# Two graph layers on one core: watched sums on GpSimd, the last fold and bias placed anew, the adjacency turned on VectorE

## The chip, the cores and the metric

The kernel runs on one core of a Trainium2 chip. The core has five engines with instruction queues of their own: TensorE (PE) multiplies matrices into PSUM, VectorE (DVE), ScalarE (ACT) and GpSimd (POOL) work elementwise, and SyncE (SP) issues all the transfers here. Each engine takes its instructions strictly in the order in which they were written; semaphores order the engines among each other. The metric is the device time of one launch in microseconds, the median of three runs. Times inside the profile count from the start of its span.

## The reference

There are B = 32 graphs of N = 512 nodes with D = 512 features, and one 512 x 512 adjacency of zeros and ones (symmetric here, with a full diagonal). Layer 0 is attention with 8 heads of 64, masked by the adjacency; layer 1 sums over neighbours and applies a weight. Both end in a residual and a layer norm.

```python
# layer 0, per graph
q, k, v = (x @ W + b for W, b in ((Wq, bq), (Wk, bk), (Wv, bv)))   # 8 heads of 64
scores = q @ k.T / 8 + where(adj == 0, -1e9, 0)
x = layernorm(x + softmax(scores) @ v)
# layer 1
y = adj @ x
x = layernorm(x + y @ weight + bias)
```

Everything is float32.

## The kernel before, in words

A fast kernel does the whole work and keeps a verdict; a slow general kernel runs only if the verdict says that an input was out of the fast kernel's range (sums of exponentials or their reciprocals too large, or an adjacency that a shortened number format doesn't hold exactly). With these inputs it doesn't run.

*Products.* Each 512 x 512 x 512 product is done by Strassen's scheme in 2 x 2 blocks of 256 with seven block products (`project` for q, k and v, `convolve` for layer 1, all through `block_product`, L350). Their factors are blocks or sums of blocks of the weights (`sum_weights`, L302: T1 = B12 - B11, T2 = B22 - T1, T3 = B22 - B12, T4 = B21 - T2) and of the activations (`combine_rows`, L315, on GpSimd but for the first graph). `ORDER` gives the order of the products: 1, 5, 6, 7, 2, 3, 4. The layer-1 products take 1, 2, 5, 6, 7, 3, 4.

*Attention.* Heads go in groups of four, two groups a graph, in pairs hp. `scores` (L558) makes transposed scores, VectorE adds the mask from `gap` (1 where the adjacency is zero) on the way out of PSUM (L560), ScalarE takes the exponential (L562), and GpSimd adds up the exponentials of a pair (L573). `attend` (L582) multiplies with the values. `fold_squares` turns the sums of exponentials in 32 x 32 squares and reduces them (L619, L621), a store and four loads through DRAM bring the partial sums to the right partitions (L626, L633), and `add_up` (L638 to L641) makes the sums and their reciprocals; it also adds both to the running tiles `sums` (VectorE) and `inverses` (GpSimd) for the verdict.

*Layer 1.* `split` cuts the normalised rows into a high and a low half[...] (L438 on ScalarE, L442 on VectorE), and adds the bias of layer 1 to the rows on GpSimd (L443). `aggregate` (L469) multiplies with `adjT`. For the last graph `split_rows` (L488, L489), `add_bias` (L492) and `aggregate_rows` (L501, L506, L508) do this by rows.

*Order.* There is no planner. The main loop writes `attend` and `scores` for each group and then a hand-made list of units (`units_of`, L756): the projections of graph b+1 and the layer-1 work of b-1, with small work of the other engines merged behind each product. For the last graph the first slot holds the layer-1 products of graph 29 with statistics, normalisation, splits and the first fold of the last group behind them (L770); the second slot begins with the second fold and its loads (L771). After the loop stands the end: `add_up`, `last_residual`, the products of graph 30 (`rest`) with the statistics, normalisation and row splits of graph 31 between them, the statistics of graph 29 (`older`), the bias of graph 31, `judge` (L668, the verdict's operands), the aggregation of graph 31, its products (`last`) and the stores of the last rows.

*Start.* Seven matmuls on a zero tile come first. x of graph 0 comes in four transfers, Wq in two column halves of 512 KB (L256), then Wk, held back by a copy on ScalarE (L695), the adjacency in one transfer (L700), Wv, the rows of graph 1 in 16 transfers of squares (L250), x again, the layer-1 weight and x of graph 1. `adjacency(c)` transposes four 128 x 128 blocks on TensorE into PSUM (L284), copies them to `adjT` on ScalarE (L285) and fills `gap` on VectorE (L286).

Of the kernel before, what the change touches and what calls it, by code (L numbers as in the profile page):

```python
# [37 lines left out]
FP = mybir.dt.float32  # L38
# [26 lines left out]
def load_row(nc, pool, v, name):  # L65
    t = pool.tile([P, v.shape[0]], FP, name=name)
    nc.sync.dma_start(t, bass.AP(tensor=v.tensor, offset=v.offset, ap=[[0, P], [1, v.shape[0]]]))
    return t
# [139 lines left out]
def fast_kernel(ctx: ExitStack, tc, verdict, x, adj, Wq, bq, Wk, bk, Wv, bv, W1, b1, out):  # L208
# [16 lines left out]
    def bank(*shape):  # L225

        return psum.tile([P, *shape], FP, name="bank", tag="bank", bufs=8)
# [15 lines left out]
    def load_squares(b):  # L243


        for d in range(DB):
            IN[b, d] = work.tile([P, N // SQ, SQ], FP, name="xin", bufs=XIN)
            for i in range(P // SQ):
                cols = x[b, :, d * P + i * SQ:d * P + (i + 1) * SQ]
                nc.sync.dma_start(IN[b, d][i * SQ:(i + 1) * SQ, :, :], cols.rearrange("(j r) f -> r j f", r=SQ))  # L250
# [10 lines left out]
    wq = load_factors(Wq, "wq")  # L261
# [9 lines left out]
    sums = consts.tile([P, NB, GROUP], FP, name="sums")  # L271
    inverses = consts.tile([P, NB, GROUP], FP, name="inverses")
    nc.gpsimd.memset(sums, 0.0)
    nc.gpsimd.memset(inverses, 0.0)
# [6 lines left out]
    def adjacency(c):  # L281
        pt = bank(NB, P)
        for m in range(NB):
            nc.tensor.transpose(pt[:, m, :], adj_s[:, c, m * P:(m + 1) * P], ident)  # L284
        nc.scalar.activation(adjT[:, :, c * P:(c + 1) * P], pt, AF.Copy)  # L285
        nc.vector.tensor_scalar(gap[:, :, c * P:(c + 1) * P], pt, 0.0, None, op0=ALU.is_equal)  # L286

    def look_for_low_half(c):

        kept = work.tile([P, N], FR, name="high")  # L290
        nc.scalar.activation(kept, adj_s[:, c, :], AF.Copy)
        cut = work.tile([P, N], FP, name="attT")
        nc.vector.tensor_tensor(cut, adj_s[:, c, :], kept.bitcast(FP), op=ALU.not_equal)
        nc.vector.tensor_reduce(inexact[:, c:c + 1], cut, axis=AX.X, op=ALU.add)
# [145 lines left out]
    def split_low(b, d):  # L440
        cols = X[b][:, :, d * P:(d + 1) * P]
        nc.vector.tensor_sub(LOW[b, d], cols, HIGH[b, d].bitcast(FP))  # L442
        nc.gpsimd.tensor_add(cols, cols, b1_r[:, None, d * P:(d + 1) * P].to_broadcast([P, NB, P]))  # L443
# [191 lines left out]
    def add_up(b, g):  # L635

        inverse = INVERSE[b, g] = work.tile([P, NB, GROUP], FP, name="inverse")
        nc.vector.tensor_reduce(inverse, PART.pop((b, g)).rearrange("p a c h -> p c h a"), axis=AX.X, op=ALU.add)  # L638
        nc.vector.tensor_add(sums, sums, inverse)  # L639
        nc.vector.reciprocal(inverse, inverse)  # L640
        nc.gpsimd.tensor_add(inverses, inverses, inverse)  # L641
# [26 lines left out]
    def judge():  # L668
        seen = consts.tile([P, 3], FP, name="seen")
        nc.vector.tensor_reduce(seen[:, 0:1], sums, axis=AX.XY, op=ALU.add)  # L670
        nc.vector.tensor_reduce(seen[:, 1:2], inverses, axis=AX.XY, op=ALU.add)
        nc.vector.tensor_reduce(seen[:, 2:3], inexact, axis=AX.X, op=ALU.add)
        well = consts.tile([P, 3], FP, name="well")
        nc.vector.tensor_scalar(well[:, 0:2], seen[:, 0:2], BOUND, None, op0=ALU.is_le)
        nc.vector.tensor_scalar(well[:, 2:3], seen[:, 2:3], 0.0, None, op0=ALU.is_equal)
        nc.vector.tensor_mul(well[:, 0:1], well[:, 0:1], well[:, 1:2])
        nc.vector.tensor_mul(well[:, 0:1], well[:, 0:1], well[:, 2:3])
        return well[:, 0:1]
# [20 lines left out]
    adj_s = work.tile([P, NB, N], FP, name="yT", bufs=1)  # L699
    nc.sync.dma_start(adj_s, adj.rearrange("(c p) m -> p c m", p=P))  # L700
    wv = load_factors(Wv, "wv")
    bv_r = load_row(nc, consts, bv, "bv_r")
    if B > 1:
        load_squares(1)
# [17 lines left out]
    combine(wv, bv_r)  # L722
    for c in range(NB):
        adjacency(c)
        run(first[9 + c:10 + c])
    run(first[13:16])
# [29 lines left out]
    def units_of(b):  # L756
# [7 lines left out]
        if b == B - 1:  # L764


            first, second = folds(b, 1)
            fetched = [(fetch_parts, b, 1)]
            behind = [fresh[:2], fresh[2:], young[:1] + scaled[:1], young[1:3], young[3:5] + [first],
                      young[5:] + splits[:1], splits[1:] + scaled[1:]]  # L770
            return [merge(convolution(b - 2), behind), [second] + fetched + added + gathered]  # L771
# [64 lines left out]
    run(rest[:1])  # L836
    for c in range(NB):
        statistics(t, 0, c)
    ahead = norm(t, 0)
    run(ahead[:1] + rest[1:2] + ahead[1:2])  # L840
    for c in range(NB):
        run(ahead[2 + c:3 + c])
        split_rows(t, c)
        run(rest[2 + c:3 + c])
    run(rest[2 + NB:])
    older, seen = survey(t - 2), survey(t - 1)
    run(older)
    for c in range(NB):
        add_bias(t, c)
# [53 lines left out]
    store(t, [2, 3])  # L903
# [24 lines left out]
```

## Time and profile before

| | us |
|---|---|
| median of 3 runs | 2744.57 (2743.18 to 2746.03) |
| the profiled execution's own time | 2743.55 |
| its span | 2741.70 |
| PE busy in the span | 2720.6 |
| DVE busy | 2145.6 |
| POOL busy | 1914.2 |
| ACT busy | 1411.0 |

A line of the timeline reads: start, length, engine, source line, operation, output from input, shapes, how many in a row; in brackets how long the engine stood idle before it and what released it. A line of the waits reads: the engine and tile that waited, for whom, microseconds in total, how often, the longest. PEld is the loading of TensorE's stationary operand. The granted clock is TensorE's, 1.00 at full speed. A matmul of float32 appears as two records.

### The profile page before, as it was taken

Reading aid. Unit: us, or ns where it says so; the run is one execution under the profiler, and the core shown is the slowest. Engines: PE = TensorE matmul, PEld = TensorE weight load, DVE = VectorE, ACT = ScalarE, POOL = GpSimd, SP = SyncE. Lnnn points to the kernel's source line nnn. Section 1 sums busy time; section 2 is a strip of 40 time slices with the busy share of each in tenths; the row PEclk is TensorE's granted clock in tenths of the full one; section 3 lists DMA queues with packets and bytes.
Section 4 is the critical chain, followed back from the end, with each engine's and each line's share of the span. In section 5 each row is a group of like instructions: output and inputs, shape, how many; then the busy total and the mean of one; then the engine's idle time right before and its main releaser. Section 6 shows DMA issues by size and latency. Waiting matters only on the chain.

```text
span 2741.7 us, 36328 instructions
## 1 busy us (share of the span) xinstructions
PE 2720.6 (99%) x12344; PEld 1903.7 (69%) x12344; DVE 2145.6 (78%) x3540; ACT 1411.0 (51%) x2459; POOL 1914.2 (70%) x1221
## 2 busy tenths in 40 slices
PE   9999999999999999999999999999999999999997
PEld 6676676766766767667677676676776766767765
DVE  6878778788787787877877778778778787787787
ACT  3455464555544655545545455464465544655554
POOL 4776677766867667777677766686766867767774
PEclk9999999999999999999999999999999999999998
DMA  5223231233221332212323123331233222332121
GB/s 159 49 36 79 69 74 36 60 79 75 67 44 56 75 79 63 54 51 71 79 67 63 45 64 79 71 71 39 61 76 77 65 48 55 72 79 64 48 63 48
DMA packets 632927, 179.16 MB, mean 65 GB/s; under 512 B 578464, under 2 KB 582560, under 8 KB 632736
## 3 DMA queue, kind: packets, MB, share of 16 engines
q1 hardware_dynamic: 632736, 176.79, 27.3%
q8 instruction: 99, 1.62, 0.2%
q14 instruction: 92, 0.75, 0.1%
HBM read 108.01 MB, written 68.68 MB: 64 GB/s over the span
## 4 chain that ended last, share of the span: by engine, by line
PE 96%; DVE 2%; DMA 0%; ACT 0%; POOL 0%; issue 0%; SPq 0%; DVEq 0%; ACTq 0%
PE bank L350 56%; PE bank L558 17%; PE bank L582 16%; PE bank L469 8%; DVE bnst L412 0%; DVE e L560 0%; DMA wq<-in_L_gnn_Wq_dram 0%; DVE xs L531 0%; DVE xT L531 0%; DVE k L442 0%; POOL xs L529 0%; ACT xs L427 0%; DVE sums L639 0%; DVE stat L413 0%; DVE part L861 0%
## 5 line engine op out<-in xcount | busy, mean ns | idle before, releaser
L562 ACT ACTIVATE e<-e 128x1024 f32<-128x1024 f32 x512 | 524.9, 1053 | 575.2 <-DVE e L560 539.9
L573 POOL TENSOR_TENSOR es<-e 128x1024 f32<-128x1024 f32 x128 | 316.5, 2473 | 481.1 <-ACT e L562 481.1
L560 DVE SCALAR_TENSOR_TENSOR e<-gap,bank 128x512 f32<-128x512 uint8 x1024 | 617.7, 678 | 20.2 <-PE bank L558 20.2
L573 POOL TENSOR_TENSOR es<-es,e 128x1024 f32<-128x1024 f32 x256 | 618.9, 2418 | 20.1
L558 PE MATMUL bank<-q,k 64*128 64x512 f32 x2048 | 463.7, 598 | 0.0
L582 PE MATMUL bank<-e,v 128*64 128x512 f32 x2048 | 453.6, 595 | 0.0
L350 PE MATMUL bank<-wv,xT 128*128 128x256 f32 x1792 | 405.4, 381 | 0.0
L350 PE MATMUL bank<-xT,wk 128*128 128x256 f32 x1792 | 402.8, 379 | 0.0
L350 PE MATMUL bank<-xT,wq 128*128 128x256 f32 x1792 | 400.8, 381 | 1.2 <-DMA wq<-in_L_gnn_Wq_dram 1.0
L350 PE MATMUL bank<-w,yT 128*128 128x256 f32 x1792 | 392.6, 379 | 2.7 <-DVE yT L506 2.7
L350 PEld LDWEIGHTS bank<-wv,xT 128*128 128x128 f32 x1792 | 337.7, 190 | 70.2 <-DVE e L560 24.3
L350 PEld LDWEIGHTS bank<-xT,wq 128*128 128x128 f32 x1792 | 337.8, 190 | 69.9 <-DVE e L560 23.5
L558 PEld LDWEIGHTS bank<-q,k 64*128 64x128 f32 x2048 | 203.8, 186 | 258.3 <-issue 147.8
L350 PEld LDWEIGHTS bank<-w,yT 128*128 128x128 f32 x1792 | 340.1, 190 | 51.4 <-DVE yT L506 3.1
L350 PEld LDWEIGHTS bank<-xT,wk 128*128 128x128 f32 x1792 | 340.2, 190 | 46.1
L652 ACT ACTIVATE rows<-rows,zero,inverse 128x64 f32<-128x64 f32 x1008 | 343.1, 426 | 2.1 <-DVE inverse L640 2.1
L582 PEld LDWEIGHTS bank<-e,v 128*64 128x64 f32 x2048 | 141.3, 137 | 277.1 <-issue 275.7
L562 ACT ACT_TABLE_LOAD x30 | 38.5, 1283 | 406.1 <-DVE e L560 406.1
L442 DVE TENSOR_TENSOR low<-xs,high 128x512 fp32r<-128x512 f32 x122 | 163.1, 1337 | 61.5 <-ACT high L438 61.5
L531 DVE TENSOR_TENSOR xs<-bank,xs 128x512 f32<-128x512 f32 x186 | 124.3, 683 | 96.6 <-PE bank L350 57.2
L427 ACT ACTIVATE xs<-xs,shift,rstd 128x512 f32<-128x512 f32 x248 | 181.9, 803 | 32.0 <-DVE shift L422 21.3
L443 POOL TENSOR_TENSOR xs<-xs,b_r 128x512 f32<-128x512 f32 x124 | 157.4, 1282 | 21.5 <-DVE low L442 21.5
(125 smaller groups left out, 3013.0 us busy)
## 6 DMA issues: line engine op xcount, KB each, us to landing
turned<-attT SPq DMA_DIRECT2D x126, 256.0 KB, 2.0
rows<-turned SPq DMA_DIRECT2D x504, 64.0 KB, 2.5
xin<-in_x_dram SPq DMA_DIRECT2D x496, 64.0 KB, 2.4
xs<-in_x_dram SPq DMA_DIRECT2D x31, 1024.0 KB, 5.2
out_dram<-xs SPq DMA_DIRECT2D x31, 1024.0 KB, 4.4
part<-passed SPq DMA_DIRECT2D x256, 8.0 KB, 1.8
passed<-part SPq DMA_DIRECT2D x64, 32.0 KB, 1.5
xin<-in_x_dram SPq DMA_DIRECT2D x4, 256.0 KB, 3.2
```

The source lines that it names most:

```text
L350: nc.tensor.matmul(pm[:, r, :], left[:, d, r * P:(r + 1) * P], right[:, d, :], start=(d == 0), stop=(d == 1))
L427: nc.scalar.activation(row, row, AF.Identity, bias=SHIFT[t][:, slot:slot + 1], scale=RSTD[t][:, slot:slot + 1])
L442: nc.vector.tensor_sub(LOW[b, d], cols, HIGH[b, d].bitcast(FP))
L443: nc.gpsimd.tensor_add(cols, cols, b1_r[:, None, d * P:(d + 1) * P].to_broadcast([P, NB, P]))
L469: nc.tensor.matmul(pm.rearrange("p a n -> p (a n)"), part, adjT[:, n % NB, :], start=(n == 0), stop=(n == 2 * NB - 1))
L531: nc.vector.tensor_add(block, pm, block)
L558: nc.tensor.matmul(ps[s], keys[:, j * P:(j + 1) * P], queries, start=True, stop=True)
L560: nc.vector.scalar_tensor_tensor(e[:, s, :], gap[:, j, :], NEG * root, ps[s], op0=ALU.mult, op1=ALU.add)
L562: nc.scalar.activation(e, e, AF.Exp, scale=1.0 / root)
L573: nc.gpsimd.tensor_add(ES[b, hp], ES[b, hp] if j > 1 else E[b, hp, 0], E[b, hp, j])
L582: nc.tensor.matmul(po[s * HD:(s + 1) * HD, :], values, e[:, s, :], start=(j == 0), stop=(j == NB - 1))
L652: nc.scalar.activation(part, part, AF.Identity, bias=zero, scale=inverse[:, c, s:s + 1])
```

## The change

- `wq` is loaded in four blocks of 256 x 256, in the order B11, B12, B22, B21, in place of two halves.
- The adjacency is loaded as 32 x 32 squares in 16 transfers, as the rows of graph 1 are, and behind Wv and its bias instead of ahead of them. `adjacency(c)` turns a block with one VectorE transpose from SBUF to SBUF; ScalarE and VectorE read that tile. TensorE's sixteen transposes go. One projection unit goes ahead of the first block where the first block stood ahead of it.
- `add_up` puts sum and reciprocal side by side in one tile, and one GpSimd addition adds both to a tile `watched` in place of the two tiles.
- For graph 30 the bias is no longer added in `split_low`, but after the last group's statistics, by rows.
- The second fold of the last group and its loads stand between the second and the third split of graph 30. They stood behind all the layer-1 products of graph 29.
- At the end the first product of graph 30 is written behind the statistics and that bias; `older` and graph 31's bias are spread among the row splits; `judge` reduces both watched rows in one operation and combines the three comparisons by a minimum in place of two multiplications.
- Of the last two row blocks the fourth is stored first.

```diff
+    def place_squares(t, rows, d):
+        for i in range(P // SQ):
+            cols = rows[:, d * P + i * SQ:d * P + (i + 1) * SQ]
+            nc.sync.dma_start(t[i * SQ:(i + 1) * SQ, :, :], cols.rearrange("(j r) f -> r j f", r=SQ))
...
-    wq = load_factors(Wq, "wq")
+    wq = consts.tile([P, 7, 2, half], FP, name="wq")
+    for name, r, c in (("B11", 0, 0), ("B12", 0, 1), ("B22", 1, 1), ("B21", 1, 0)):
+        nc.sync.dma_start(wq[:, B_AT[name], :, :], Wq[r * half:(r + 1) * half, c * half:(c + 1) * half].rearrange(
+            "(c p) f -> p c f", p=P))
...
     def adjacency(c):
-        pt = bank(NB, P)
-        for m in range(NB):
-            nc.tensor.transpose(pt[:, m, :], adj_s[:, c, m * P:(m + 1) * P], ident)
-        nc.scalar.activation(adjT[:, :, c * P:(c + 1) * P], pt, AF.Copy)
-        nc.vector.tensor_scalar(gap[:, :, c * P:(c + 1) * P], pt, 0.0, None, op0=ALU.is_equal)
+        turned = work.tile([P, N], FP, name="attT")
+        nc.vector.transpose(turned, adj_s[:, c, :, :].rearrange("p j f -> p (j f)"))
+        nc.scalar.activation(adjT[:, c, :], turned, AF.Copy)
+        nc.vector.tensor_scalar(gap[:, c, :], turned, 0.0, None, op0=ALU.is_equal)
...
         nc.vector.tensor_sub(LOW[b, d], cols, HIGH[b, d].bitcast(FP))
-        nc.gpsimd.tensor_add(cols, cols, b1_r[:, None, d * P:(d + 1) * P].to_broadcast([P, NB, P]))
+        if b != B - 2:
+            nc.gpsimd.tensor_add(cols, cols, b1_r[:, None, d * P:(d + 1) * P].to_broadcast([P, NB, P]))
...
     def add_up(b, g):
-        inverse = INVERSE[b, g] = work.tile([P, NB, GROUP], FP, name="inverse")
-        nc.vector.tensor_reduce(inverse, PART.pop((b, g)).rearrange("p a c h -> p c h a"), axis=AX.X, op=ALU.add)
-        nc.vector.tensor_add(sums, sums, inverse)
-        nc.vector.reciprocal(inverse, inverse)
-        nc.gpsimd.tensor_add(inverses, inverses, inverse)
+        both = work.tile([P, 2, NB, GROUP], FP, name="inverse")
+        total, inverse = both[:, 0, :, :], both[:, 1, :, :]
+        nc.vector.tensor_reduce(total, PART.pop((b, g)).rearrange("p a c h -> p c h a"), axis=AX.X, op=ALU.add)
+        nc.vector.reciprocal(inverse, total)
+        nc.gpsimd.tensor_add(watched, watched, both)
+        INVERSE[b, g] = inverse
...
     def judge():
-        nc.vector.tensor_reduce(seen[:, 0:1], sums, axis=AX.XY, op=ALU.add)
-        nc.vector.tensor_reduce(seen[:, 1:2], inverses, axis=AX.XY, op=ALU.add)
+        nc.vector.tensor_reduce(seen[:, 0:2], watched.rearrange("p k c h -> p k (c h)"), axis=AX.X, op=ALU.add)
...
-        nc.vector.tensor_mul(well[:, 0:1], well[:, 0:1], well[:, 1:2])
-        nc.vector.tensor_mul(well[:, 0:1], well[:, 0:1], well[:, 2:3])
-        return well[:, 0:1]
+        nc.vector.tensor_reduce(well[:, 3:4], well[:, 0:3], axis=AX.X, op=ALU.min)
+        return well[:, 3:4]
...
-    adj_s = work.tile([P, NB, N], FP, name="yT", bufs=1)
-    nc.sync.dma_start(adj_s, adj.rearrange("(c p) m -> p c m", p=P))
     wv = load_factors(Wv, "wv")
     bv_r = load_row(nc, consts, bv, "bv_r")
+    adj_s = work.tile([P, NB, N // SQ, SQ], FP, name="yT", bufs=1)
+    for c in range(NB):
+        place_squares(adj_s[:, c, :, :], adj, c)
...
+    run(first[9:10])
     for c in range(NB):
         adjacency(c)
-        run(first[9 + c:10 + c])
-    run(first[13:16])
+        run(first[10 + c:11 + c])
+    run(first[14:16])
...
-                      young[5:] + splits[:1], splits[1:] + scaled[1:]]
-            return [merge(convolution(b - 2), behind), [second] + fetched + added + gathered]
+                      young[5:] + splits[:1], splits[1:2] + [second] + fetched + splits[2:] + scaled[1:]]
+            return [merge(convolution(b - 2), behind), added + gathered]
...
-    run(rest[:1])
     for c in range(NB):
         statistics(t, 0, c)
+    for c in range(NB):
+        add_bias(t - 1, c)
+    run(rest[:1])
     ahead = norm(t, 0)
     run(ahead[:1] + rest[1:2] + ahead[1:2])
+    older, seen = survey(t - 2), survey(t - 1)
     for c in range(NB):
         run(ahead[2 + c:3 + c])
         split_rows(t, c)
+        if c == 0:
+            add_bias(t, c)
+        if c == 2:
+            run(older[:2])
         run(rest[2 + c:3 + c])
-    run(rest[2 + NB:])
-    older, seen = survey(t - 2), survey(t - 1)
-    run(older)
-    for c in range(NB):
-        add_bias(t, c)
+        if c > 0:
+            add_bias(t, c)
+    run(rest[2 + NB:] + older[2:])
     well = judge()
...
-    store(t, [2, 3])
+    store(t, [3, 2])
```

## The prediction

> **What bounds the kernel now.** I read the page first. Its first part says who is busy, and the waits of TensorE (PE) say how much of the rest can be won.
>
> ```profile
> PE 2720.6 (99%) x12344; PEld 1903.7 (69%) x12344; DVE 2145.6 (78%) x3540; ACT 1411.0 (51%) x2459; POOL 1914.2 (70%) x1221
> ```
>
> ```profile
> PE bank L501 <- DVE low L489: 3.2, 1, 3.2
> PE bank L350 <- DVE yT L506: 2.7, 1, 2.7
> PE bank L690 <- DVE attT L687: 1.1, 1, 1.1
> PE bank L350 <- DMA wq<-in_L_gnn_Wq_dram: 1.0, 1, 1.0
> PE bank L469 <- DVE low L442: 0.8, 1, 0.8
> PE bank L350 <- DVE wq L302: 0.2, 1, 0.2
> ```
>
> PE never waits between about 11 us and 2679 us. So edits that run in the 32 loops (the sums moved to GpSimd) are worth nothing there: PE hides them. What the change can win or lose lies in the first 45 us and the last 65 us. I took the timeline of both. Start:
>
> ```profile
> 8.30 1.97 PE L350 MATMUL bank<-xT,wq 128*128 128x256 f32 x8 [0.97 <-DMA wq<-in_L_gnn_Wq_dram]
> 9.75 0.69 DVE L302 TENSOR_TENSOR wq<-wq 128x512 f32<-128x512 f32 x1 [1.33 <-DMA wq<-in_L_gnn_Wq_dram]
> 10.49 7.17 PE L350 MATMUL bank<-xT,wq 128*128 128x256 f32 x32 [0.23 <-DVE wq L302]
> 38.34 7.21 PE L558 MATMUL bank<-q,k 64*128 64x512 f32 x32
> ```
>
> End (the third line is one of 1.1 us pieces in which a tiny VectorE (DVE) operation waits for GpSimd (POOL)):
>
> ```profile
> 2681.50 3.48 DVE L442 TENSOR_TENSOR k<-xs,k 128x512 fp32r<-128x512 f32 x2
> 2692.18 0.26 DVE L638 TENSOR_REDUCE inverse<-part 128x16 f32<-128x64 f32 x1 [3.50 <-DMA part<-passed]
> 2692.47 1.09 DVE L639 TENSOR_TENSOR sums<-sums,inverse 128x16 f32<-128x16 f32 x1
> 2703.79 0.77 PE L501 MATMUL bank<-adjT,low 128*128 128x512 f32 x1 [3.24 <-DVE low L489]
> 2715.45 1.19 DVE L677 TENSOR_TENSOR well<-well 128x1 f32<-128x1 f32 x1
> 2716.56 0.68 DVE L506 COPY yT<-bank 128x512 f32<-128x512 f32 x1
> 2717.30 8.47 PE L350 MATMUL bank<-w,yT 128*128 128x256 f32 x38 [2.72 <-DVE yT L506]
> ```
>
> The chain of waits runs through DVE almost without a break from 2692 to 2717: parts arrive, add_up, last_residual, statistics, low halves, judge, L506. DVE is the bound of the end, not PE.
>
> **What the Trainium skill says.** "TensorE: Matmul & The Clock Gate", Part 1: the array falls to half clock after an idle window of about 3.4 us. The trace agrees: after the 3.24 us wait the granted clock reads 0.50 from 2704 to 2709, and L501 takes 0.43 us a matmul instead of 0.24. "SBUF — State Buffer", SBUF: two separate sides: VectorE with two SBUF inputs and GpSimd share a port pair that one holds for a whole instruction. The trace agrees: L442 takes 0.69 us at best and 1.48 in the median, L676 and L677 take 1.18 for one element. "VectorE: DVE Perf Modes", The three transpose paths: VectorE turns 32x32 blocks only, hence the loading by squares; L335, the same operation here, takes 0.70.
>
> **The change, part by part** (times of the profiled execution; its own time is 2743.55, span 2741.70).
>
> *Queries' weights by blocks.* Two transfers of 512 KB become four of 256 KB. The halves landed at about 8.25 and 9.65, 1.4 us per 512 KB, so B11, B12, B22, B21 land at about 7.55, 8.25, 8.95, 9.65 (estimate from these). The first product starts at 7.6 instead of 8.30. T1 needs B12 and DVE is free at 8.41, so it ends at 9.1; the second product follows the first (1.75 us each) at 9.35 instead of 10.49: **−1.14**. The third needs T2, DVE's third operation, at 10.3; it is due at 11.1. SP issues two more transfers of 0.43 us, but the keys' weights wait for ScalarE at 7.45 anyway.
>
> *Adjacency turned on DVE.* PE loses 16 transposes, 0.44 us for each group of four in the chain: **−1.76**. DVE gains four transposes (0.70 at most, 0.61 back to back). Its line from the last q product: four wv sums and bv_r to 27.1, then nine evacuations and fills of gap as before plus four transposes at about 0.61 each, ending near 35.5, where PE delivers the last k product (35.5) and starts the scores. So the extra work just fits. But gap is now filled from SBUF (between 0.54, L901's time, and 0.68 as from PSUM), and L381 and L382 of GpSimd (1.27 each) run just then: two fills may wait up to 1.3 each. Scores need the last k columns 1.7 us after they start, and DVE must not be over 0.6 late for the eight banks: I take **+0.3**, between 0 and 2.7. The 16 square transfers stand on SP ahead of 16 for x, load, w1 and b1. In the trace 16 of the same shape took from 13.57 to about 30.2, behind a backlog with the 1 MB adjacency in it. Now they are issued from about 12 and should land by 25 (estimate); DVE wants the last at 33. The x squares then land near 33 to 46 at worst; DVE wants them at 58.66. Hidden.
>
> *Sums and reciprocals on GpSimd.* 64 L639 (mean 0.58) go, 64 GpSimd additions of 16 columns (L641, 0.224) become 64 of 32 columns: between 0.224 and twice that, I take 0.24, since L641 is nearly all fixed cost beside 1.27 for 512 columns. Each waits, as before, for DVE's reciprocal. Hidden by PE; without that cover 64 x 0.58 = 37 us would be won on DVE. Only the last two count, below.
>
> *The last fold.* It was behind both last splits; now it is ahead of them. For the upper part: L639 gone at 2667.6 (1.78) lets shift end before GpSimd's L529 rather than behind it, so normalise starts near 2673.3 (2675.34), the first low half is ready at 2677.9, and PE goes from L582 (ends 2679.06) straight on: −0.75. The second fold (1.24 + 2 x 0.64) then runs 2679.1 to 2681.6, and its parts land 4.73 later as before: 2686.3 instead of 2692.18. Low halves 2 and 3 follow; without the four bias additions (L443) beside them they take 0.69, but two L656 of GpSimd can delay each once: third low half at 2682.4 to 2683.7, wanted by PE at 2682.9. So the aggregation ends at 2687.0 (2686.7 to 2687.5) against 2687.42, and add_up, now behind L474's last, at 2688.3 instead of 2692.18: **−3.9**.
>
> *From add_up to normalise* the old distance is 9.27. L639 goes (−1.1); the bias of b=30 now stands on GpSimd behind three L315 and the watched addition, which itself waits for the reciprocal; its four operations of 1.25 end at 2697.4, so the tiny shift may wait for it (+1.0, 0 to 1.2). x11's sum needs its first two, done at 2694.8, where DVE arrives: no wait. Normalise at 2697.5. Low half 0 at 2699.7; PE ends the convolution at 2700.3: the wait of 3.24 is gone, and with it the half clock.
>
> *From normalise to L506* the old distance is 15.1. Two of the older statistics fill the 1.17 wait for GpSimd (L527). judge takes 0.75 instead of 3.2, as two 1.2 us multiplications become one reduction and the additions of bias are spread earlier; one small comparison may still wait (+0.6, up to 1.2). Sum 12.1: L506 at 2709.7 to 2710.2: **−6.5** in all at this point (I take the later). PE's new wait there is about 1.5 us, too short for the half clock (2.72 was). From there DVE's work is unchanged. *Store order:* row 3 is ready 0.44 before row 2: **−0.3**, 0 to 0.45.
>
> Sum: −1.14 −1.76 +0.3 −6.5 −0.3 = **−9.4**. Own time 2743.55 − 9.4 = 2734.2; the median shown is 1.0 above this execution: **2735.2**.
>
> **Rivals.** *Tail half won.* The fold ahead of low halves 2 and 3 holds PE at L469 up to 1.7, GpSimd's bias delays shift and judge at their worst (1.2 each), low halves lose 1.3: the tail gives about 3 instead of 6.5, total 6: 2738.7. For it: L442's median of 1.48. Against: fewer GpSimd operations stand there. *DVE overfull at the adjacency.* gap waits at both L381 and L382, and the scores stall by 2.4: 2737.6. For it: L302 on wk took 1.0 each beside L382. *Slower: squares late.* If block 3's last square landed at L, everything behind on DVE is late and PE loses L − 33.8. At L above 40.5 this and the half clock (2.8 more) eat all gains; at 46 the time is 2750. Against it: 30.2 with more ahead. *It doesn't do what it says:* the parts don't set the end once they are early, because L474 does; that is in my sum already.
>
> **How the numbers follow.** Forecast 0.62 (2733 to 2737.5), tail half won 0.22, DVE overfull 0.13, squares late 0.03. The bounds taken together (start −3.2 to −0.2, tail −8 to −4) with 1.5 us between runs give 2732.8 to 2739.5. A measurement of this kernel tells about 0.2%, 5.5 us, from no change: below 2739.1 lies all of the forecast but little, and most of the two milder rivals: 0.85; within 0.12; slower 0.03.
>
> **What would show it.** Right: no wait of PE for Wq over 0.3; scores starting near 35.5; add_up near 2686 (the start's 2.6 off); granted clock 1.0 in the last aggregation; judge under 1.3. Wrong: a wait of PE for e at 36 to 45, a wait over 1.5 of the aggregation of b=30 for a low half, PE idle over 3 us ahead of the last aggregation, or add_up early but the copy into yT (L506) not.

## The result: 11 us less, at the low edge of what was forecast

| | before | after |
|---|---|---|
| median (6 runs each, on one chip) | 2743.99 us (2743.18 to 2746.49) | 2733.03 us (2732.30 to 2734.60) |
| the profiled execution's own time | 2743.55 | 2732.94 |
| its span | 2741.70 | 2731.10 |

The ratio is 0.9959, 95% interval 0.9947 to 0.9971: faster by 0.41%, and the interval lies clear of 1. The forecast was 2735.2, range 2732.8 to 2739.5; by the ratio (0.9959 x 2743.99 = 2732.7) the change comes out just below the range, by its median just inside. The sign and the main places were right, and the gain was forecast too small; the section "The prediction, step by step" says which steps failed.

### The profile page after: what moved, and what is told of

It is laid out like the page before. It is cut to its first block, busy times and chain, and to the rows that moved or that the text cites. A ratio compares the mean times of both kernels' runs of the same rounds, so it can differ in the third digit from the quotient of the medians.

```text
span 2731.1 us, 36264 instructions
## 1 busy us (share of the span) xinstructions
PE 2716.7 (99%) x12328; PEld 1900.6 (70%) x12328; DVE 2104.9 (77%) x3478; ACT 1411.3 (52%) x2459; POOL 1915.0 (70%) x1220
## 4 chain that ended last, share of the span: by engine, by line
PE 97%; DVE 1%; POOL 0%; ACT 0%; DMA 0%; issue 0%; SPq 0%; DVEq 0%; ACTq 0%; POOLq 0%
PE bank L355 56%; PE bank L564 17%; PE bank L588 16%; PE bank L475 8%; POOL es L579 0%; DVE xs L537 0%; DVE bnst L417 0%; DVE e L566 0%; DMA xin<-in_x_dram 0%; DVE part L627 0%; DVE v L625 0%; DVE part L874 0%; DVE mix L533 0%; DVE k L447 0%; ACT xT L432 0%
## 5 line engine op out<-in xcount | busy, mean ns | idle before, releaser
L566 DVE SCALAR_TENSOR_TENSOR e<-gap,bank 128x512 f32<-128x512 uint8 x1024 | 617.7, 678 | 20.2 <-PE bank L564 20.2
L564 PE MATMUL bank<-q,k 64*128 64x512 f32 x2048 | 463.3, 598 | 0.0
L588 PE MATMUL bank<-e,v 128*64 128x512 f32 x2048 | 453.6, 595 | 0.0
L355 PE MATMUL bank<-wv,xT 128*128 128x256 f32 x1792 | 405.4, 381 | 0.0
L355 PE MATMUL bank<-xT,wk 128*128 128x256 f32 x1792 | 402.4, 379 | 0.0
L355 PE MATMUL bank<-xT,wq 128*128 128x256 f32 x1792 | 400.5, 381 | 0.8 <-ACT xT L331 0.8
L355 PE MATMUL bank<-w,yT 128*128 128x256 f32 x1792 | 394.2, 380 | 1.9 <-DVE yT L512 1.9
L355 PEld LDWEIGHTS bank<-wv,xT 128*128 128x128 f32 x1792 | 337.6, 190 | 70.1 <-DVE e L566 24.3
L355 PEld LDWEIGHTS bank<-xT,wq 128*128 128x128 f32 x1792 | 337.8, 190 | 69.1 <-DVE e L566 23.5
L564 PEld LDWEIGHTS bank<-q,k 64*128 64x128 f32 x2048 | 203.6, 186 | 258.1 <-issue 146.5
L355 PEld LDWEIGHTS bank<-w,yT 128*128 128x128 f32 x1792 | 341.2, 191 | 50.8 <-DVE yT L512 2.3
L355 PEld LDWEIGHTS bank<-xT,wk 128*128 128x128 f32 x1792 | 340.5, 190 | 46.3
L588 PEld LDWEIGHTS bank<-e,v 128*64 128x64 f32 x2048 | 141.4, 137 | 277.1 <-issue 275.1
L447 DVE TENSOR_TENSOR low<-xs,high 128x512 fp32r<-128x512 f32 x122 | 161.7, 1325 | 91.1 <-ACT high L443 91.1
L478 ACT ACTIVATE yT<-bank 128x512 f32<-128x512 f32 x124 | 74.2, 599 | 187.0 <-PE bank L475 187.0
```

Source lines behind the costliest of these rows:

```text
L355: nc.tensor.matmul(pm[:, r, :], left[:, d, r * P:(r + 1) * P], right[:, d, :], start=(d == 0), stop=(d == 1))
L478: nc.scalar.activation(yt[:, d // 2:d // 2 + 3:2, d % 2, :], pm, AF.Copy)
L564: nc.tensor.matmul(ps[s], keys[:, j * P:(j + 1) * P], queries, start=True, stop=True)
L566: nc.vector.scalar_tensor_tensor(e[:, s, :], gap[:, j, :], NEG * root, ps[s], op0=ALU.mult, op1=ALU.add)
L588: nc.tensor.matmul(po[s * HD:(s + 1) * HD, :], values, e[:, s, :], start=(j == 0), stop=(j == NB - 1))
```

## The profile after

The change moves most lines of code by five or six: L355 is the block product (L350 before), L564 the scores (L558), L566 the mask (L560), L475 the aggregation (L469), L447 the low halves (L442), L645 and L646 `add_up` (L638, L640), L625 and L627 the fold (L619, L621), L507 and L512 the last aggregation and its copy (L501, L506). L288 and L290 are new.

First part of the page of the kernel after, then the waits of TensorE (tile and line that waited, for whom, microseconds in all, how often, longest):

```profile
PE 2716.7 (99%) x12328; PEld 1900.6 (70%) x12328; DVE 2104.9 (77%) x3478; ACT 1411.3 (52%) x2459; POOL 1915.0 (70%) x1220
```

```profile
PE bank L355 <- DVE yT L512: 1.9, 1, 1.9
PE bank L695 <- DVE attT L692: 1.1, 1, 1.1
PE bank L355 <- ACT xT L331: 0.8, 1, 0.8
PE bank L475 <- DVE k L447: 0.2, 1, 0.2
PE bank L329 <- DMA xin<-in_x_dram: 0.2, 1, 0.2
```

The waits for both kinds of low half (3.2 and 0.8) are gone but for 0.2, and so in this profile is the one for Wq. The copy into yT still makes PE wait, for 1.9 instead of 2.7. These lists differ by 4.8 us; the span by 10.6. The rest lies where this list doesn't reach: sixteen transposes fewer, a clock that is no longer halved in the last aggregation (0.50 from 2704 to 2709 before, 1.00 from 2694 to 2704 after), stalls of PE on full banks (below), and the stretch behind PE's last matmul.

The start, from the timeline of the kernel after (start, length, engine, line, operation, how many in a row, and in brackets the idle time before):

```profile
7.72 8.87 PE L355 MATMUL bank<-xT,wq 128*128 128x256 f32 x40 [0.77 <-ACT xT L331]
...
28.54 0.43 DVE L290 TENSOR_SCALAR gap<-attT 128x512 uint8<-128x512 f32 x1
...
30.22 1.05 DVE L290 TENSOR_SCALAR gap<-attT 128x512 uint8<-128x512 f32 x1
...
35.52 7.21 PE L564 MATMUL bank<-q,k 64*128 64x512 f32 x32
36.68 1.88 DVE L566 SCALAR_TENSOR_TENSOR e<-gap,bank 128x512 f32<-128x512 uint8 x3 [0.26 <-PE bank L564]
```

From its first product to the scores PE shows no wait, and DVE stands idle for 0.26 us before it gets the first scores to mask: its four transposes and fills of `gap` fit in. Of the four fills three took 0.43 and one 1.05.

The end:

```profile
2675.56 1.24 DVE L625 STREAM_TRANSPOSE v<-es 128x1024 f32<-128x1024 f32 x1
...
2678.03 2.42 DVE L447 TENSOR_TENSOR k<-xs,k 128x512 fp32r<-128x512 f32 x2
...
2684.64 0.42 DVE L480 TENSOR_TENSOR yT<-bank,yT 128x256 f32<-128x256 f32 x1 [1.44 <-ACT yT L478]
2684.98 0.25 DVE L645 TENSOR_REDUCE inverse<-part 128x16 f32<-128x64 f32 x1
...
2693.28 0.73 DVE L427 SCALAR_TENSOR_TENSOR shift<-stat,rstd 128x4 f32<-128x4 f32 x1
...
2706.10 0.16 DVE L682 TENSOR_REDUCE well<-well 128x1 f32<-128x3 f32 x1
2706.17 0.68 DVE L512 COPY yT<-bank 128x512 f32<-128x512 f32 x1
2706.91 10.16 PE L355 MATMUL bank<-w,yT 128*128 128x256 f32 x38 [1.93 <-DVE yT L512]
```

The last fold (2675.56) now stands ahead of the last two low halves, and `add_up` (2684.98) no longer waits for its parts but follows L480 at once. The shift waits 0.57 us (0.73 instead of its usual 0.16). After the copy PE's 38 matmuls take 10.16 us where 38 took 8.47 before; the windows by the microsecond show why (the number after the engines is the granted clock):

```profile
2707.00:2708.00 1.00, 1.00 (x5) 0.90 (x6) 1.00 (x3) 0.00 (x0) 0.21 (x1) 0.97 0.00 0
2708.00:2709.00 1.00, 1.00 (x4) 0.83 (x3) 0.11 (x1) 0.09 (x1) 0.74 (x1) 0.50 0.00 0
2709.00:2710.00 1.00, 1.00 (x4) 0.73 (x4) 0.39 (x1) 0.69 (x2) 1.00 (x2) 0.50 0.00 0
2710.00:2711.00 1.00, 1.00 (x4) 0.82 (x3) 0.97 (x4) 0.20 (x1) 1.00 (x2) 0.50 0.00 0
2711.00:2712.00 1.00, 1.00 (x6) 0.83 (x5) 0.97 (x3) 1.00 (x2) 0.98 (x1) 0.83 0.00 0
```

## The experiments

Whole times of one kernel spread by up to 4 us, partly because the first transfers do: the first scores of graph 0 begin between 35.24 and 37.15 us in kernels whose code up to there is the same. So I read each profile in stages: from those scores to the last `add_up`, on to graph 31's first normalised rows (`norm`), to the copy into yT, to the last normalised rows, to the end of the span. Each stage is the difference of two starts in the timeline. Where nothing in a stage was edited it repeats closely: seven kernels have 12.07 to 12.09 to the copy.

| kernel | scores at | to add_up | to norm | to copy | to last rows | to end | median |
|---|---|---|---|---|---|---|---|
| before | 38.34 | 2653.84 | 9.27 | 15.11 | 18.31 | 6.83 | 2743.99 |
| after | 35.52 | 2649.46 | 9.12 | 12.07 | 18.39 | 6.54 | 2733.03 |
| start_only | 35.80 | 2653.95 | 9.26 | 15.11 | 18.31 | 6.77 | 2742.09 |
| adjacency_on_tensor | 37.16 | 2649.38 | 9.11 | 12.08 | 18.31 | 6.26 | 2734.98 |
| fold_late | 35.66 | 2650.72 | 8.56 | 12.09 | 19.53 | 6.54 | 2733.94 |
| sums_on_vector | 35.36 | 2650.87 | 9.75 | 12.07 | 18.33 | 6.52 | 2736.15 |
| fold_and_sums | 36.06 | 2653.23 | 9.38 | 12.07 | 18.32 | 6.24 | 2737.02 |
| bias_at_split | 35.33 | 2649.17 | 8.53 | 12.09 | 18.32 | 6.66 | 2732.62 |
| two_products | 37.15 | 2649.53 | 9.11 | 13.25 | 19.54 | 6.32 | 2734.60 |
| looks_early | 35.57 | 2648.05 | 9.11 | 12.07 | 18.31 | 6.49 | 2732.01 |
| older_early | 36.00 | 2649.39 | 9.11 | 9.56 | 18.53 | 6.41 | 2731.26 |
| older_looks | 35.24 | 2648.13 | 9.12 | 9.57 | 18.53 | 7.01 | 2729.49 |
| older_looks_bias | 35.81 | 2647.75 | 8.53 | 9.97 | 18.12 | 6.42 | 2728.31 |

Before ran again beside each group of them, with medians of 2743.99 to 2745.17. The groups ran on different chips, so a difference of about 1 us between medians of different groups tells nothing by itself; the stages have to carry it. Of each kernel one execution was profiled. All these kernels do the whole computation. They carry the changed kernel's line numbers, shifted by a few at most.

The stage to `add_up` holds the loops and the beginning of the tail. From PE's last `attend` (L582, L588) to `add_up` it is 20.21 before, 16.21 after, 17.33 in `fold_late`, 17.07 in `sums_on_vector`, 19.36 in `fold_and_sums` and 15.77 in `bias_at_split`; what is left of a difference lies in the loops.

### The start alone

The kernel before with the new start: Wq by blocks, the adjacency by squares and turned on DVE.

```diff
-    wq = load_factors(Wq, "wq")
+    wq = consts.tile([P, 7, 2, half], FP, name="wq")
+    for name, r, c in (("B11", 0, 0), ("B12", 0, 1), ("B22", 1, 1), ("B21", 1, 0)):
+        nc.sync.dma_start(wq[:, B_AT[name], :, :], ...)
...
+        nc.vector.transpose(turned, adj_s[:, c, :, :].rearrange("p j f -> p (j f)"))
```

> The kernel before with the start alone: Wq in four blocks and the adjacency turned on VectorE; the rest of the change is left out. My theory: the start is worth 2.8 us (scores begin at 35.5 instead of 38.34) and does nothing to the end, so 2741.2 with before at 2744.0, and PE still waits about 3.2 us for the low half and 2.7 us for the copy into yT. Rival: what PE gains at the start is lost again where VectorE is behind anyway; then the scores begin early and the time stays within 1 us of before.

Measured: 2742.09 (2740.59 to 2743.37), ratio 0.9990 (0.9983 to 0.9996). The scores begin at 35.80 (−2.54), and every later stage is that of before within 0.11. The gain at the start is carried through 2.7 ms almost whole, and by itself it moves nothing at the end. About 8 of the 10.6 us have to come from the other edits.

### The adjacency back on TensorE

Its load in one transfer ahead of Wv comes back with it.

```diff
-        turned = work.tile([P, N], FP, name="attT")
-        nc.vector.transpose(turned, adj_s[:, c, :, :].rearrange("p j f -> p (j f)"))
...
+        pt = bank(NB, P)
+        for m in range(NB):
+            nc.tensor.transpose(pt[:, m, :], adj_s[:, c, m * P:(m + 1) * P], ident)
...
-    run(first[9:10])
     for c in range(NB):
         adjacency(c)
-        run(first[10 + c:11 + c])
-    run(first[14:16])
+        run(first[9 + c:10 + c])
+    run(first[13:16])
```

> The changed kernel with the adjacency as it was before: one transfer ahead of Wv, four TensorE transposes a block. Wq by blocks stays. Measured on TensorE from the start of its first q product to the first q.k scores, which leaves out when the first x arrives: 27.80 us in the changed kernel, 30.04 before (2.19 of that stretch to its second product). Theory A (the prediction's terms, its stall of 0.3 on VectorE dropped because none was seen): the sixteen transposes cost 1.76, the stretch is 29.5 to 29.6, and the time 1.7 to 1.8 more, 2734.3 to 2735.3. Theory B (the prediction as it stood, with 0.3 us of VectorE's work not hidden): 29.2 to 29.3.

The two lines that bound the stretch, from its timeline:

```profile
7.60 6.71 PE L356 MATMUL bank<-xT,wq 128*128 128x256 f32 x30 [1.08 <-DMA wq<-in_L_gnn_Wq_dram]
...
37.16 7.21 PE L565 MATMUL bank<-q,k 64*128 64x512 f32 x32
```

37.16 − 7.60 = 29.56, against 27.80 (35.52 − 7.72) in the changed kernel: 1.76, the sixteen transposes as priced. The stretch is 27.79 to 27.85 in ten of the eleven profiles that share this start, and 28.59 in `two_products`, where x came late. The median rose by 1.95. Theory A holds; there was nothing of DVE's work that wasn't hidden. What is left of the stretch, 30.04 − 29.56 = 0.48, goes to the second product, which no longer waits for T1. The first product's own start (8.30 to 7.72) makes up the rest of the 2.82 in this pair of profiles, but it lies between 7.39 and 8.56 in the twelve profiles with these loads of Wq.

### The last fold back behind the products

```diff
-                      young[5:] + splits[:1], splits[1:2] + [second] + fetched + splits[2:] + scaled[1:]]
-            return [merge(convolution(b - 2), behind), added + gathered]
+                      young[5:] + splits[:1], splits[1:] + scaled[1:]]
+            return [merge(convolution(b - 2), behind), [second] + fetched + added + gathered]
```

> The changed kernel with the second fold back behind the splits and the products; all else stays. Rival (as the prediction's sum has it): the fold's place is what brings add_up 3.9 us forward, so this costs about 3.9 us (2736.9). My theory after the trace of after: with the sums off VectorE and the bias out of the splits, the low halves end so early that the parts land at about 2685.9 even then, against add_up at 2684.98, which the last yT addition sets; so it costs only 0.7 to 1.5 us (2734.0), and PE's 0.2 us wait for low half 2 goes.

Measured: `add_up` 1.26 later, and it waits for its parts again (first line below); 0.56 of that comes back, since the shift finds GpSimd done. The median is 2733.94, 0.9 more. The 1.14 in the stage after the copy goes with the halved clock of this execution, which set in earlier than in the changed kernel's (see the prediction's steps); its time, 2734.95, is also 1 us above the other three. The second theory holds: by itself the fold's place is worth about 1 us, not the 3.9 that stands beside it in the prediction.

```profile
2686.38 0.26 DVE L645 TENSOR_REDUCE inverse<-part 128x16 f32<-128x64 f32 x1 [1.48 <-DMA part<-passed]
```

### The running sums back on VectorE

```diff
-        nc.vector.reciprocal(inverse, total)
-        nc.gpsimd.tensor_add(watched, watched, both)
+        nc.vector.tensor_add(sums, sums, inverse)
+        nc.vector.reciprocal(inverse, inverse)
+        nc.gpsimd.tensor_add(inverses, inverses, inverse)
```

> The changed kernel with the old add_up: the sums are added up on VectorE again, in all 64 groups. Theory: 62 of the 64 are hidden behind PE, but for 0.3 us at the scores of graph 1, where VectorE is behind; the last two cost: the one of the first group of graph 31 delays shift and with it the low halves by up to 1.8 us, of which PE shows about 0.5; the last one stands in the chain and waits for GpSimd, 0.3 to 1.2. Sum +1.2 to +2.5 us, 2735.0. Rival: all of VectorE's 37 us count, or a tenth of it (+3.7); second rival: nothing, because the chain has room elsewhere.

Measured: 2736.15 (2734.70 to 2736.61); `add_up` 1.41 later, 0.55 of it in the loops and 0.86 behind the last `attend`, and norm another 0.63. Together that is 2.0, as expected. The profiled execution is the fastest of seven; the median lies 3.1 above the changed kernel's, and the stages don't show where the other 1.1 went. The same pieces of DVE's timeline, of this kernel and then of the changed one:

```profile
2664.82 1.76 DVE L647 TENSOR_TENSOR sums<-sums,inverse 128x16 f32<-128x16 f32 x1
...
2670.91 1.25 DVE L429 SCALAR_TENSOR_TENSOR shift<-stat,rstd 128x4 f32<-128x4 f32 x1
2672.17 0.69 DVE L535 TENSOR_TENSOR mix<-bank,mix 128x512 f32<-128x512 f32 x1
```

```profile
2668.72 0.16 DVE L427 SCALAR_TENSOR_TENSOR shift<-stat,rstd 128x4 f32<-128x4 f32 x1
2670.09 0.69 DVE L533 TENSOR_TENSOR mix<-bank,mix 128x512 f32<-128x512 f32 x1 [1.21 <-POOL xs L535]
```

An addition of 16 columns holds DVE for 1.76 us, and by that delay the shift falls into another GpSimd operation and takes 1.25 instead of 0.16. Without it the shift comes before that operation. The 0.63 is the last such addition (1.18 at 2686.51), less the 0.57 that the shift of the changed kernel waits.

### Both together

The fold late and the sums on DVE, the two diffs above in one kernel.

> The changed kernel with two of its edits undone together: the second fold and its loads behind all products of graph 29 again, and the running sums added by VectorE again (as before the change). Singly these two delayed the start of add_up by 1.3 and 1.4 us, measured from the start of the first q.k scores. Theory A (one line): both stand ahead of the store of the parts on the same line of VectorE, and singly each hid in the 1.8 us that VectorE waits for L480's evacuations. Then together they cost more than their sum: VectorE reaches the last fold at 2681 to 2681.5 and the parts land 4.6 us after its end, so add_up starts 3.5 to 4.0 us later than in the changed kernel and the time is 2737.5 to 2739. Theory B (sum of parts): add_up 2.7 us later, time 2736 to 2737.3.

Measured: `add_up` 3.77 later, 2737.02 (2736.22 to 2737.99).

```profile
2678.73 3.48 DVE L449 TENSOR_TENSOR k<-xs,k 128x512 fp32r<-128x512 f32 x2
2682.13 1.23 DVE L627 STREAM_TRANSPOSE v<-es 128x1024 f32<-128x1024 f32 x1
...
2689.29 0.26 DVE L646 TENSOR_REDUCE inverse<-part 128x16 f32<-128x64 f32 x1 [2.74 <-DMA part<-passed]
```

Singly 1.26 and 1.41 (2.67 together), in one kernel 3.77, inside theory A's 3.5 to 4.0: both stand on one line of DVE ahead of the parts, and singly each of them hides partly in DVE's waits for L480's evacuations (2.32 and 1.44 in the changed kernel). A's 3.5 to 4.0 left out the loops, which hold 0.62 of the 3.77; behind the last `attend` it is 3.15, still far more than the 1.12 and 0.86 that each costs there alone. The median is 0.5 below what A gave and inside B's range; the stages decide for A. This is the tail's main gain, 3.15 of 4.00; neither edit owns it. Who owns the last 0.85 no run shows: the second low half takes 0.68 here and took 1.40 before, beside GpSimd's bias, so the bias's move is the likely one.

### Graph 30's bias back in its splits

```diff
-        if b != B - 2:
-            nc.gpsimd.tensor_add(cols, cols, ...)
+        nc.gpsimd.tensor_add(cols, cols, ...)
...
-    for c in range(NB):
-        add_bias(t - 1, c)
     run(rest[:1])
```

> The changed kernel with the bias of graph 30 added in the splits again and not after the statistics. Theory: GpSimd's four additions stand beside the low halves again, these take 1.3 to 1.7 us, PE waits about 1.3 us for them in the aggregation of graph 30; given back 0.6 us, because the small shift operation of graph 31 no longer waits for GpSimd. Sum +0.7 us (0 to 1.6; 2733.7). Rival: the bias is the heart of the early add_up and its way back costs 3 us or more (2736).

A miss: `add_up` is 0.29 earlier, not later, and norm another 0.59, for the shift doesn't wait (below). The low halves beside the additions did take longer in one place (1.39 for the second), but shorter in another: the last two took 1.28 together instead of 2.42, for in the changed kernel GpSimd, freed of the additions, is at its next large operation (L663, 2676.75 to 2679.3) just then, and here only at 2682.34. The median, 2732.62, is 0.4 less. In the changed kernel, with its early fold, moving this bias brought nothing; by these two stages it cost 0.9.

```profile
2692.79 0.16 DVE L427 SCALAR_TENSOR_TENSOR shift<-stat,rstd 128x4 f32<-128x4 f32 x1
```

### The verdict by products instead of a minimum

```diff
-        nc.vector.tensor_reduce(well[:, 3:4], well[:, 0:3], axis=AX.X, op=ALU.min)
+        nc.vector.tensor_mul(well[:, 0:1], well[:, 0:1], well[:, 1:2])
+        nc.vector.tensor_mul(well[:, 0:1], well[:, 0:1], well[:, 2:3])
```

> The changed kernel with judge's two one-element multiplications again instead of the minimum, at the same place. Theory: VectorE's chain sets the end, and a multiplication waits for the GpSimd operation that runs (bias products of graph 30 until 2707.2); the second finds GpSimd free. So the copy into yT and the end come 1.2 us later (2734.2). Rivals: the full old price, 2.4 us, or nothing, if PE and not VectorE set the end.

```profile
2707.75 1.17 DVE L682 TENSOR_TENSOR well<-well 128x1 f32<-128x1 f32 x1
2708.96 0.16 DVE L683 TENSOR_TENSOR well<-well 128x1 f32<-128x1 f32 x1
```

The stage to the copy is 13.25 instead of 12.07: +1.18, as expected, and not the rivals' 2.4 or 0. The first multiplication ends at 2708.92, with the GpSimd operation that runs beside it (L540, 2707.64 to 2708.91); the reduction in its place (0.16) doesn't wait. Of the 3.0 that this stage lost through the change, 1.2 is this. The other 1.8 goes by subtraction to the rest of `judge` (3.14 to 1.08 in all) and to the older statistics in the place of a 1.17 us wait; no run took these apart.

### The looks moved: is PE stalled without a recorded wait?

The changed kernel gains 0.4 us between the first scores and the last attend, where the list of PE's waits shows nothing in either kernel. Most of it lies at one group of scores, the first of graph 2, which stands in graph 1's turn (the expectation calls it graph 1's). PE and DVE there in the kernel before, then after:

```profile
169.45 8.45 PE L558 MATMUL bank<-q,k 64*128 64x512 f32 x32
171.88 8.42 DVE L560 SCALAR_TENSOR_TENSOR e<-gap,bank 128x512 f32<-128x512 uint8 x14
```

```profile
166.62 8.13 PE L564 MATMUL bank<-q,k 64*128 64x512 f32 x32
168.74 7.82 DVE L566 SCALAR_TENSOR_TENSOR e<-gap,bank 128x512 f32<-128x512 uint8 x13
```

In graph 0 32 such records take 7.21. Here DVE starts to empty their banks 2.43 (2.12 after) behind the first matmul, and PE takes 1.24 (0.92) longer. The loads of PE's weights show what holds it. They have a list of their own; here are those ahead of the last eight of these records, after the change:

```profile
171.83 0.29 PEld L564 LDWEIGHTS bank<-q,k 64*128 64x128 f32 x2 [0.30 <-DVE e L566]
172.43 0.29 PEld L564 LDWEIGHTS bank<-q,k 64*128 64x128 f32 x2 [0.30 <-DVE e L566]
173.03 0.29 PEld L564 LDWEIGHTS bank<-q,k 64*128 64x128 f32 x2 [0.30 <-DVE e L566]
173.62 0.29 PEld L564 LDWEIGHTS bank<-q,k 64*128 64x128 f32 x2 [0.30 <-DVE e L566]
```

They come every 0.60 us, each 0.05 behind the end of a mask, where the first matmuls of the group came every 0.43. The kernel has eight banks, and the last load follows the eighth mask. The experiment takes the cause of DVE's lateness away: the four looks for a low half of the adjacency (a comparison of 0.68 to 2.13 and a reduction of 0.69 each) go from graph 1's first slot to graph 0's.

```diff
         elif b:
             behind = [ready + fresh] + [[u] for u in young]
-            behind += [[(look_for_low_half, c)] for c in range(NB)]
         else:
             behind = [[]] + [[(sum_weights, w1, n)] for n in range(4)]
+            behind += [[(look_for_low_half, c)] for c in range(NB)]
```

> The changed kernel with the four looks for the low half of the adjacency moved from the first slot of graph 1 to the first slot of graph 0. Theory: the scores of graph 1 take 8.06 us instead of 7.14 because VectorE comes late to them and the banks are not free, a stall that the list of PE's waits doesn't show; moved to graph 0, where VectorE has little else, it goes: -0.9 us (2732.1). Rival: the stall only moves to graph 0's scores, 0.

```profile
166.67 7.21 PE L564 MATMUL bank<-q,k 64*128 64x512 f32 x32
167.83 8.46 DVE L566 SCALAR_TENSOR_TENSOR e<-gap,bank 128x512 f32<-128x512 uint8 x14 [0.33 <-PE bank L564]
```

DVE now waits for PE, the scores take 7.21, and the stage to `add_up` is 1.41 shorter, more than the 0.9 expected; 0.92 of it is this stall; the other 0.5 comes in steps of a few hundredths spread over all the later loops, and its cause is open. So PE was held by full banks, and DVE's lateness filled them. The kernel with the sums on DVE fits in between: mask 2.31 behind (169.12 against 166.81), scores 8.32. The length follows the mask's lag by the hundredth (lags 2.12, 2.31, 2.43; lengths 8.13, 8.32, 8.45).

A second group is held too, the last scores of graph 1, one group earlier: 8.31 before, after and in `looks_early`, with a lag of 2.30, and 8.65 or 8.66 with a lag of 2.65 in `start_only` and `sums_on_vector`. The same rule fits it (the length is the lag plus 6.0), and nothing here removes it.

### The older statistics earlier

After the change DVE idles 2.3 and 1.4 us in the aggregation of graph 30 and 1.59 ahead of graph 31's first low half, while the four statistics of graph 29 (eight operations) and the verdict's operands stand on its line to the copy. The statistics go into the gaps of that aggregation, the verdict's operands to where the first two of them stood.

```diff
-            return [merge(convolution(b - 2), behind), added + gathered]
+            aged = survey(b - 2)
+            return [merge(convolution(b - 2), behind),
+                    added + gathered[:2] + aged[:3] + gathered[2:3] + aged[3:] + gathered[3:]]
...
-    older, seen = survey(t - 2), survey(t - 1)
+    seen = survey(t - 1)
...
         if c == 2:
-            run(older[:2])
+            well = judge()
...
-    run(rest[2 + NB:] + older[2:])
-    well = judge()
+    run(rest[2 + NB:])
```

> The changed kernel with the four statistics of graph 29 (3.2 us of VectorE) moved from between the row splits to the gaps of VectorE during the aggregation of graph 30, and judge into the place where VectorE waits for GpSimd. Theory: VectorE's chain sets the end, so the copy into yT comes 2.2 us earlier relative to normalise, until the last aggregation itself ends; end 2.4 us earlier (2730.6), PE's wait of 1.9 us for the copy falls below 0.3. Rival: the chain behind the copy is bound elsewhere (GpSimd's three sums, stores), and the end moves under 1 us.

Measured: 9.56 to the copy instead of 12.07 (−2.51), nothing lost ahead of it, PE's wait for yT gone; 2731.26 (2730.82 to 2732.16).

### Together: a kernel faster than both

The last two edits in one kernel:

> Both of the last two edits. If they are independent, -3.3 us against the changed kernel: 2729.7. If the looks only move the stall, -2.4.

Measured: 2729.49 (2729.20 to 2730.03), ratio to before 0.9946 (0.9930 to 0.9963); the two gains add up, as expected of independent ones (2729.7). With the bias of graph 30 back in its splits too:

> The changed kernel with three edits of mine: four of the older statistics inside the aggregation of graph 30 and the verdict's operands in VectorE's wait for GpSimd, the four looks for a low half of the adjacency in the first slot of graph 0, and the bias of graph 30 added in its splits again (as before the change). Theory A (the bias moved by the change brings nothing, and leaves VectorE's tiny shift waiting for GpSimd by 0.6): 0.4 to 0.6 us below the version without the third edit, about 2729.0. Theory B (that gain needs the slack that the first two edits use up): no difference, 2729.2 to 2730.

Measured: 2728.31 (2728.06 to 2728.63), ratio 0.9940 (0.9924 to 0.9957), 4.7 us below the changed kernel (4.8 by the stages). Norm comes 0.59 earlier and 0.40 of it is given back in the stage to the copy, where DVE now waits 0.50 for PE: TensorE is the bound there again. The fall of 1.2 in the median is more than the expected 0.4 to 0.6. In the stages 0.38 comes ahead of `add_up`, as in `bias_at_split`, and 0.41 behind the copy, which isn't assigned.

## The prediction, step by step

In the profiled pair the span fell by 10.60, against a sum of 9.4. Two steps failed: the loops, priced at nothing, gave 0.38, because PE was held at full banks there; and the tail up to the copy was put at 6.5 and gave 7.19. In stages: start −2.82, to `add_up` −4.38, to norm −0.15, to the copy −3.04, after it −0.21.

*Queries' weights by blocks (−1.14): half of it shown.* −0.48 for the second product holds in the stretch behind the first product's start. The −0.58 for the first product can't be told from chance: its start spreads over 1.2 us in twelve profiles, and before has a single one. In this profile the wait for Wq is gone and one for x, 0.77, shows in its place, which the sum had not seen; in four of the other eleven PE still waits for Wq, by 1.1 in `adjacency_on_tensor`.

*Adjacency on DVE (−1.76 + 0.3): the gain right, the stall wrong.* The transposes cost 1.76 as priced. DVE's line ended at 36.4 rather than 35.5, but with 0.26 to spare at the mask: nothing stalled. The term "+0.3" measured 0. The fills from SBUF took 0.43, less than the 0.54 to 0.68 taken, and of the two feared waits for GpSimd one came (1.05). The last square's load was issued by 25.65 and none made DVE wait: the rival "squares late" and the rival "DVE overfull" are both out.

*"Edits that run in the 32 loops are worth nothing there": the step that failed in kind.* It was drawn from PE's list of waits. The PE held by full banks here isn't in that list; it shows as a long group of matmuls, and in the weight loads. From the first scores to the attend at 2671.97 (2668.77 after) PE gained 0.38, 0.32 of it at the first scores of graph 2. The runs assign it over the two held groups: 8.31 and 8.45 before, 8.65 and 8.34 with the new start alone, 8.31 and 8.13 after. So the new start made them 0.23 longer in all, and the sums' move took 0.55 back, as it does undone alone (8.66 and 8.32, 0.54 more). That is what the term at nothing is worth.

*The last fold (−3.9): right in size, its cause named too narrowly.* Relative to the loops `add_up` came 4.00 earlier, behind L480's last as said. But the working put it to the fold and counted L639 as a help. Behind the last `attend` the two, undone singly, cost 1.12 and 0.86, and together 3.15. The part on PE was right: −0.75 forecast for the aggregation's start, −0.83 measured (with the sums back on DVE, PE waits 0.73 there again); −0.4 for its end, −0.41 measured. The bias out of the splits, which was to speed up the low halves, brought nothing in the changed kernel.

*From add_up to norm (9.27 to 9.2): right in sum, with luck.* It took 9.12. L639's 1.09 went as said and the shift waited 0.57 where 1.0 was taken, which leaves 8.75; another 0.37 in small gaps on DVE, which the sum did not have, made up the difference.

*To the copy (15.1 to 12.1): right, 12.07; the sum "−6.5" up to there: the step that failed in size.* It was taken near the later end of a range of 0.5. The steps themselves give 3.9 + 0.07 + 3.0 = 7.0, and 7.19 was measured. Taking the later end cost 0.5 of the 1.2 that the sum was short; the start's 0.2 and the loops' 0.4 are most of the rest.

*"Too short for the half clock": wrong, at no price here.* PE's wait was 1.93 and its clock was halved for some 3.4 us soon after it. The stage after the copy still took 18.39, against 18.31 with full clock before. That was luck. The halving began 1.8 us behind the copy, so ScalarE emptied the first product only 0.41 later than before (2.74 behind the copy against 2.33), and the shift that follows on DVE waited 0.40 less for GpSimd (0.35 against 0.75). In `fold_late` and `two_products` it began 0.9 and 1.2 behind the copy, the first product came 1.24 and 0.94 later, and the stage took 1.2 more.

*Store order (−0.3).* The last stage is 0.29 shorter, but it ranges from 6.24 to 7.01 in kernels that share this end, so the profile shows nothing for it either way. It had no run of its own.

*The rival "tail half won"* is out: the tail gave 7.4, not 3.

*The range.* The prediction's bounds, −11.2 to −4.2 on 2744.57, added up with 1.5 us on either side, give 2731.9 to 2741.9; it stated 2732.8 to 2739.5, which is narrower than its own working at both ends.

*From the sum to the median.* 1.0 was added because the median shown was that far above the profiled execution. In these six runs before is 0.44 above it and the changed kernel 0.09. So of the 2.2 between 2735.2 and 2733.03, 1.2 is the sum and the rest is this.

## What to carry to other kernels

PE's list of waits did not show here that its output banks were full: compare the length of the same group of matmuls between stages, and look at the weight loads, before calling other engines' work free. Two delays on one line ahead of a slack have to be undone together to be priced; singly each of them hides in the slack of the other's absence. And when each step of a sum has a middle, don't take the pessimistic end of one step silently: it was the largest single error of the sum here.

## What the runs showed of the hardware

*The halved clock isn't settled by the wait's length.* PE's wait for the copy was 1.93 us in the changed kernel and in `fold_late`, with the clock halved for about 3.4 us after it, and 1.93 in `looks_early` and 1.92 in `adjacency_on_tensor`, with full clock throughout; before the change 2.72 did not halve it either. The Trainium skill, "TensorE: Matmul & The Clock Gate", Part 1, names an idle window of about 3.4 us and says that the window runs freely, so that effects vary from run to run. The first doesn't describe these runs, where 1.93 was enough in two profiles and 2.72 was not in a third; the second fits, though none of these runs shows the window itself. What decides stays open.

*Who waits for GpSimd.* In DVE's tail the tiny additions and products of two SBUF operands took up to 1.76 where 0.16 is usual, and the long ones end with the GpSimd operation beside them: L647 of `sums_on_vector` at 2666.58 (GpSimd 2666.55), the shift after the change at 2694.01 (2693.99), L682 of `two_products` at 2708.92 (2708.91). TENSOR_REDUCE (0.15 and 0.16) and the statistics (0.66 to 0.69) did not lengthen in the same stretch, with GpSimd busy. The Trainium skill, "SBUF — State Buffer", SBUF: two separate sides, says that a DVE operation with two SBUF inputs, or in one of DVE's two-port modes, takes the port pair that it shares with GpSimd, and that the other waits. The comparisons with one input, L680 (0.73, next to 0.14 for L681) and L290 (1.05, next to 0.43), agree if they ran in such a mode, which no run here shows by itself.
